# Two bottleneck blocks in one kernel: Winograd streams that build each unit when it is due, and two more idle matmuls around each Gram stage

## The chip, the cores and the metric

The kernel runs on one core of one Trainium2 chip. The metric is the device time of one execution, in microseconds. It was taken from three runs before the change. One further execution was recorded by the hardware profiler, and all durations below come from that one unless a sentence says otherwise.

## The reference, cut to what matters

Two residual blocks follow each other. Each has three convolutions with batch normalisation over the whole batch of 64 images of 14 x 14 pixels; everything is float32.

```python
def block(x, w1, b1, g1, be1, w2, b2, g2, be2, w3, b3, g3, be3, residual_scale):
    out = relu(bn(conv(x,   w1, b1, pad=0), g1, be1))    # 1x1, 1024 -> 256 channels
    out = relu(bn(conv(out, w2, b2, pad=1), g2, be2))    # 3x3,  256 -> 256
    out =      bn(conv(out, w3, b3, pad=0), g3, be3)     # 1x1,  256 -> 1024
    return relu(x + softplus(residual_scale) * out)
x = block(x, *layer0); x = block(x, *layer1)             # x: (64, 1024, 14, 14)
```

## The kernel before, in words

Images are taken two at a time; such a pair is a tile `t`, 0 to 31, with 392 pixels per channel. The 256-channel activations stay in SBUF (`y_all`). The 1024-channel input of a block is streamed in tiles `x` (128 partitions x 8 x 392 values, 1568 KB each): from the kernel's input in block 0, from a DRAM copy `mid` in block 1.

The span has these stages, in order:

1. The first 1x1 convolution of block 0 (`first`, 0 to about 300 us). Beside it, VectorE and ScalarE transform the 3x3 filters of both blocks (`filters`), whose raw weights come by DMA (L194).
2. The 3x3 convolution of block 0 (`conv2`, about 300 to 590 us). It ends with `busy(psum, "m", 6)` on L968: six matmuls of the identity with 448 columns, whose result nobody reads. They occupy TensorE while the other engines finish the batch statistics.
3. The Gram stage of block 0 (`gram`, `conv3_stats`, about 590 to 690 us). The statistics of the third convolution come from the 256 x 256 Gram matrix of the activations, so the convolution needs no pass of its own for them. The activations are normalised in pieces by ScalarE (L546) and shifted by VectorE (L994). The first seven chunks of 256 pixels are transposed by TensorE (`by_tensor`, L1024) and copied to SBUF by VectorE (L1030); the others by DMA and VectorE.
4. The third convolution of block 0 fused with the first of block 1 (`fused`, about 690 to 1270 us).
5. The 3x3 convolution of block 1, ended by the same six idle matmuls (about 1270 to 1560 us), and its Gram stage (about 1560 to 1650 us).
6. The last third convolution with the residual sum and the stores (`final`, about 1650 us to the end).

The 1x1 convolutions use a scheme of seven block products instead of eight (class `Seven`, one object a *unit*). `p1` to `p7` are the products on TensorE. They go into PSUM banks `y`, `x`, `p` with a prefix `a` or `c` for the first or third convolution, so `cp` is the bank `p` of a third convolution. `after1` to `after7` are what VectorE, ScalarE and GpSimd do with a bank after its product. One bank `p` is used twice by one unit: `p5` starts it, `after5` adds it to the tile (L466), `p3` accumulates further into it, `after3` adds it again (L466).

`stream` (L300) interleaves the units. In the steady state TensorE does `p1` of a unit, `p3` and `p4` of the unit before, then `p6`, `p2`, `p5`, `p7` of this unit. `stream` holds one unit ahead: at the head of its loop it asks the generator for the `following` unit before the current one is done (L306), and so knows which one is the last.

The generators do work when they are asked for a unit:

- In `final` (L1141), one pair of tiles `t, t+1` has four units (q = 0 to 3). Before q = 0 the generator makes the four operand sums `ct0` to `ct3` on VectorE (`column_sums`, L423): L430, L431, L432, L433. After a unit was taken it calls `go_out` of an older one. That is a relu on VectorE (L522) and two stores of 392 KB on SyncE's queue (L525), one from each of the two tiles. After q = 1 it loads the next tiles `x` (L1159), up to tile `t + 4`. Five `x` buffers exist, so a load waits until all four stores of the tile that held the buffer have landed.
- `fused` (L1167) runs two streams in lock step, `first_convs` and `last_convs`; the latter makes the sums and loads one tile per four units.
- The first stage (L1345) loads two tiles per unit.

The order of work is partly fixed. Every matmul, the relus of `go_out` and some others are held in program order on their engine (`tc.keep_in_program_order`). Everything else, among it the additions of L466, the sums `ct` and all DMA issues, is placed by the framework's scheduler, which takes the position in the program as priority. Each engine and each DMA issuing queue then works through its list in order.

Of the kernel before, what the change touches and what calls it, by code (L numbers as in the profile page):

```python
# [45 lines left out]
CS = C // P  # L46
MS = M // P
G = 2
T = N // G
# [38 lines left out]
def bottlenecks(ctx: ExitStack, tc: tile.TileContext, x, w1s, w2s, w3s, pars, out):  # L88
# [208 lines left out]
            yield from self.p3()  # L297
            yield from self.p4()

    def stream(items, beside=lambda: None):  # L300


        before, items = None, iter(items)
        now = next(items)
        while now is not None:
            following = next(items, None)  # L306
            yield from now.p1()
            if before is not None:
                beside()
                yield from before.last()  # L310
                beside()
            else:
                yield from now.p2()
            yield from now.p6()
            if before is not None:
                before.end()
                if following is not None:
                    beside()
                    yield from now.p2()
            beside()  # L320
            yield from now.p5()
            beside()
            yield from now.p7()
            beside()
            if following is None:
                yield from now.p2()
            before, now = now, following
        yield from before.last()
        before.end()

# [225 lines left out]
    def conv2(psum, pool, b, par, aff, affine_of, stats):  # L556

        order = (1, 2), (3, 4), (NF - 1, 0)
        pairs = [(g, p) for g in range(NG) for p in order]
# [392 lines left out]
        for k in range(NG * NF):  # L952
# [12 lines left out]
            item.columns(*qs)  # L965
            finished.send(item)
            queue = queue[1:] + list(itertools.islice(made, 1))
        busy(psum, "m", 6)  # L968

    def conv3(psum, t, o, w3, tag=None):  # L970
        ps = psum.tile(tag=tag)
# [6 lines left out]
    def gram(psum, pool, homes, aff, minus_c, beside):  # L978

        g0, g1 = psum.tile(M + 1, "cp"), psum.tile(P + 1, "ap")
        zts = [pool.tile([P, CH, M + 1], FP, tag=f"zt{i}", name=f"zt{i}") for i in range(NZT)]
        for zt in zts:
            nc.gpsimd.memset(zt[:, :, M:], 1.0)
        zts = itertools.cycle(zts)

        head = 3 * CH * P
        start = FIRST * CH * P
        bounds = [0, CH * P, head, head + STEP, *range(2 * GPX, NPX + 1, GPX)]  # L990
        pieces = list(zip(bounds, bounds[1:]))

        def less(s, y):
            tc.keep_in_program_order(nc.vector.tensor_scalar(y, y, minus_c[:, s : s + 1], None, ALU.add))  # L994

        def norm_to(end):

            while pieces and pieces[0][0] < end:
                a, e = pieces.pop(0)
                for s in reversed(range(MS)):  # L1000
                    y = y_all[:, s, a:e]
                    if a == 0 and s == 1:
                        norm_vector(s, y, aff, minus_c[:, s : s + 1])
                    else:
                        norm(s, y, aff)
                        less(s, y)

        def spread(k):

            first = start + k * STEP if k else head  # L1010
            norm_to(first + STEP)
            x = homes[k % 2][:, : MS * STEP].rearrange("p (s j f) -> p s j f", s=MS, j=4)
            for i, j in itertools.product(range(4), range(4)):
                queue = nc.gpsimd if 4 * i + j in (1, 3, 6, 8, 10, 13, 15) else nc.sync
                a = first + i * RUN
                queue.dma_start(out=x[32 * i : 32 * i + 32, :, j], in_=y_all[32 * j : 32 * j + 32, :, a : a + RUN])
            return x.rearrange("p s j f -> p (s j) f")

        def by_tensor(a):
            tp = psum.tile(CH * M)  # L1020
            for c in range(CH):
                for s in range(MS):
                    tc.keep_in_program_order(
                        nc.tensor.transpose(  # L1024
                            tp[:, (c * MS + s) * P : (c * MS + s + 1) * P],
                            y_all[:, s, a + c * P : a + (c + 1) * P], ident,
                        )
                    )
            zt = next(zts)
            tc.keep_in_program_order(nc.vector.tensor_copy(zt[:, :, :M], tp.rearrange("p (c m) -> p c m", c=CH)))  # L1030
            return zt

        def by_vector(x, i):
            zt = next(zts)
            tc.keep_in_program_order(
                nc.vector.transpose(
                    zt[:, :, :M].rearrange("p b (n c) -> p b n c", c=32),
                    x[:, :, i * CH * 32 : (i + 1) * CH * 32].rearrange("p n (b r) -> p b n r", r=32),
                )
            )  # L1040
            return zt

        def pairs():

            norm_to(head)
            then = {
                1: lambda: ready.append(spread(0)),
                2: partial(norm_to, 2 * GPX),
                4: partial(norm_to, 3 * GPX),
                5: lambda: ready.append(spread(1)),  # L1050
            }
            for i in range(FIRST):
                a = i * CH * P
                yield by_tensor(a if a < head else a + STEP)
                if i in then:
                    then[i]()
            for k in range(STEPS):
                x = ready.pop(0)
                for i in range(RUN // (CH * 32)):
                    yield by_vector(x, i)  # L1060
                if k + 2 < STEPS:
                    ready.append(spread(k + 2))
            norm_to(NPX)
            for i in range(LAST):
                yield by_tensor(NPX - (LAST - i) * CH * P)

        ready = []
        total = NPX // (CH * P)
        before = None
        for k, zt in enumerate(itertools.chain(pairs(), (None,))):  # L1070
            if before is not None:
                for c in range(CH):
                    first, last = k == 1 and c == 0, k == total and c == CH - 1
                    matmul(g0, before[:, c, 0:P], before[:, c, :], start=first, stop=last)
                    matmul(g1, before[:, c, P:M], before[:, c, P:], start=first, stop=last)
            before = zt
            if k in beside:
                beside[k]()
        return g0, g1
# [61 lines left out]
    def final(psum, pool, xpool, xs, a, w3, aff):  # L1141


        units = []

        def pairs():
            for t in range(1, T - 1, 2):
                ys = [[two(t + i, s) for i in range(2)] for s in range(MS)]
                sums = column_sums(pool, ys, PX)
                for q in range(CS // 2):  # L1150
                    units.append(Conv3Pair(psum, pool, xs[t : t + 2], q, PX, ys, sums, w3, aff, out[t : t + 2]))
                    yield units[-1]

                    while len(units) > 2:
                        units.pop(0).go_out()
                    if q == 1:

                        for i in range(len(xs), min(t + 5, T)):
                            xs.append(load_x(xpool, 1, i))  # L1159

        for _ in stream(pairs()):
            pass
        for unit in units:
            unit.go_out()
        residual(psum, xs[T - 1], 1, T - 1, a, aff)

    def fused(psum, pool, xpool, xs, w1, w3, aff, par, stats, one_done):  # L1167

        def last_convs():
            for t in range(1, T):
                if t + 1 < T:
                    xs.append(load_x(xpool, 0, t + 1))
                ys = [[two(t, s)[:, i * H // 2 : (i + 1) * H // 2] for i in range(2)] for s in range(MS)]
                n = PX // 2
                sums = column_sums(pool, ys, n)
                for q in range(CS // 2):
                    yield Conv3(psum, pool, xs[t], q, n, ys, sums, w3, aff, mids[t] if q == CS // 2 - 1 else None)

        def first_convs():
            for t in range(T):
                yield Conv1(psum, pool, xs[t : t + 1], (t,), w1, par, stats, one_done)

        a, c = stream(first_convs()), stream(last_convs())
        for i in range(LAG):
            next(c)
        while True:
            more = next(a, "end"), next(c, "end")
            if more == ("end", "end"):  # L1190
                break
# [122 lines left out]
    with tc.tile_pool(name="first", bufs=1) as one, tc.tile_pool(  # L1314
        name="first_x", bufs=4
    ) as xpool, ExitStack() as scope:
        psum = Psum(scope, ["ps"], ps=4, ay=2)
# [29 lines left out]
                xs = [load_x(xpool, 0, t + i) for i in range(2)]  # L1347
                yield Conv1(psum, one, xs, (t, t + 1), w1, par[0], stats1, one_done)

        for _ in stream(items(), beside):  # L1350
            pass

    for b in range(2):
# [95 lines left out]
```

## Time and profile before

| | |
|---|---|
| median of 3 runs | 1959.65 us (1957.53 to 1960.48) |
| profiled execution, its own time | 1959.24 us |
| its span, first to last instruction | 1957.5 us |
| TensorE clock granted over the span | 0.998 |
| busy: PE, weight load, DVE, ACT, POOL | 98%, 82%, 79%, 53%, 27% |
| PE idle: 0 to 300, 300 to 590, 590 to 700 us | 1.6, 6.6, 5.2 us |
| PE idle: 700 to 1260 us | 0.0 us |
| PE idle: 1260 to 1560, 1560 to 1670, 1670 to 1957.5 us | 8.8, 4.8, 10.6 us |

PE is TensorE's matmul, DVE is VectorE, ACT is ScalarE, POOL is GpSimd, SP is SyncE, which here only issues DMAs. Idle PE is the length of the stretch less the busy time in it. A float32 matmul appears as one or more PE records, and a line of the timeline merges equal ones that follow each other: "x2" is two records. Duration and distance are two things: a matmul of 128x392 is busy for 0.49 us, but the next one starts 0.33 us after it, because they overlap.

### The profile page before, as it was taken

What the parts mean: (1) busy time and instruction counts of PE and PEld (TensorE: products, weight loads), DVE (VectorE), ACT (ScalarE), POOL (GpSimd) and SP (SyncE); (2) the same over time, 40 slices, a digit from 0 to 9 for tenths busy, and PEclk for the clock granted to TensorE, in tenths of its full rate; (3) what the DMA queues carried; (4) which work ended last, traced back from release to release, by engine and by line L of the source; (5) the groups of instructions that cost most, each with busy time, mean ns of one, the idle gap of its engine ahead of it and who ended that gap; (6) DMA issues with size and microseconds to landing.
All of it is one profiled execution on the core that took longest, in us unless ns stands there. A gap on an engine that the chain in (4) does not pass through costs nothing.

```text
span 1957.5 us, 26989 instructions
## 1 busy us (share of the span) xinstructions
PE 1919.9 (98%) x9430; PEld 1614.4 (82%) x9430; DVE 1552.4 (79%) x2491; ACT 1041.5 (53%) x2082; POOL 532.0 (27%) x638
## 2 busy tenths in 40 slices
PE   9999999999999999999999999989999999999998
PEld 5555558999997799999999999989999887555554
DVE  5778768999998667676776776699999976888786
ACT  2222214677775055555555555457777641666665
POOL 0111100000105133433433333301010051666664
PEclk9999999999999999999999999999999999999999
DMA  7766635576747634444444444257667386899997
GB/s 289 278 248 254 249 112 165 178 208 191 207 142 203 198 135 187 173 165 177 182 169 165 179 184 166 99 183 204 203 192 207 124 199 232 298 322 339 336 341 264
DMA packets 188983, 408.39 MB, mean 209 GB/s; under 512 B 24944, under 2 KB 165136, under 8 KB 172336
## 3 DMA queue, kind: packets, MB, share of 16 engines
q1 hardware_dynamic: 161728, 324.66, 48.5%
q0 software_dynamic: 21504, 30.94, 6.9%
q10 hardware_dynamic: 5616, 51.06, 6.3%
q8 instruction: 75, 1.23, 0.3%
q14 instruction: 60, 0.49, 0.1%
HBM read 263.75 MB, written 115.34 MB: 194 GB/s over the span
## 4 chain that ended last, share of the span: by engine, by line
PE 90%; DVE 7%; issue 1%; ACT 1%; DMA 1%; SPq 0%; POOL 0%; DVEq 0%
PE ay L168 17%; PE cy L168 16%; PE columns L168 13%; PE cp L168 12%; PE ap L168 10%; PE m L168 6%; PE l L168 6%; PE ax L168 4%; PE cx L168 4%; PE ps L168 1%; DVE x L466 1%; DVE ct L431 1%; DVE f L801 0%; DMA home<-y 0%; DVE ct L433 0%
## 5 line engine op out<-in xcount | busy, mean ns | idle before, releaser
L333 ACT ACTIVATE cu<-cy,scale 128x196 f32<-128x196 f32 (+1 forms) x552 | 257.7, 473 | 286.7 <-PE cy L168 279.6
L168 PE MATMUL columns<-v,ub 128*128 128x224 f32 (+1 forms) x1536 | 301.1, 337 | 0.7 <-ACT columns L760 0.7
L168 PEld LDWEIGHTS columns<-v,ub 128*128 128x128 f32 x1536 | 269.4, 188 | 4.1 <-ACT columns L760 1.2
L333 ACT ACTIVATE x<-x,shift 128x392 f32<-128x392 f32 x428 | 239.7, 613 | 55.1 <-POOL x L492 53.2
L466 DVE SCALAR_TENSOR_TENSOR x<-cp,scale,x 128x196 f32<-128x196 f32 (+1 forms) x368 | 178.1, 484 | 98.0 <-PE cp L168 96.4
L168 PE MATMUL cy<-ct,ws 128*128 128x196 f32 (+1 forms) x736 | 222.0, 383 | 1.1 <-ACT cu L333 1.1
L168 PE MATMUL ay<-at,ws 128*128 128x196 f32 (+1 forms) x752 | 209.2, 381 | 0.0
L487 POOL TENSOR_TENSOR x<-x,cu 128x196 f32<-128x196 f32 (+1 forms) x184 | 159.2, 865 | 174.1 <-ACT cu L333 162.5
L492 POOL TENSOR_TENSOR x<-x,cu 128x392 f32<-128x392 f32 x124 | 125.9, 1015 | 192.8 <-DVE x L466 188.1
L168 PEld LDWEIGHTS ay<-at,ws 128*128 128x128 f32 x752 | 136.4, 190 | 33.6 <-ACT au L333 0.5
L168 PEld LDWEIGHTS cy<-ct,ws 128*128 128x128 f32 x736 | 133.4, 190 | 36.4 <-ACT cu L333 3.8
L168 PE MATMUL m<-sums,ua 128*128 128x224 f32 (+1 forms) x752 | 147.6, 340 | 6.2 <-DVE sums L624 6.2
L168 PE MATMUL l<-diffs,ub 128*128 128x224 f32 (+1 forms) x768 | 149.7, 338 | 3.0 <-PE columns L168 2.9
L513 POOL TENSOR_TENSOR x<-x,cu 128x392 f32<-128x392 f32 x120 | 124.5, 1038 | 86.1 <-DVE x L466 79.2
L871 POOL DMA_DIRECT2D y<-f x24 | 31.1, 1532 | 412.8 <-DVE f L801 320.8
L168 PEld LDWEIGHTS l<-diffs,ub 128*128 128x128 f32 x768 | 133.6, 189 | 7.0 <-PE columns L168 5.9
L168 PEld LDWEIGHTS m<-sums,ua 128*128 128x128 f32 x752 | 132.2, 191 | 8.7 <-DVE sums L624 7.9
L466 DVE SCALAR_TENSOR_TENSOR x<-cx,scale,x 128x196 f32<-128x196 f32 (+1 forms) x184 | 89.3, 485 | 59.1 <-PE cx L168 58.2
L333 ACT ACTIVATE au<-ay 128x196 f32<-128x196 f32 (+1 forms) x141 | 53.6, 380 | 152.0 <-PE ay L168 149.3
L168 PE MATMUL cx<-y,w 128*128 128x196 f32 (+1 forms) x404 | 124.1, 392 | 0.4 <-DVE x L1130 0.4
L168 PE MATMUL cy<-y,w 128*128 128x196 f32 (+1 forms) x404 | 123.8, 392 | 0.0
L168 PE MATMUL cp<-zt 128*128 128x257 f32 x392 | 118.8, 385 | 1.8 <-DVE zt L1030 1.7
(211 smaller groups left out, 3950.1 us busy)
## 6 DMA issues: line engine op xcount, KB each, us to landing
x<-in_x SPq DMA_DIRECT2D x62, 1568.0 KB, 6.8
ub<-u SPq DMA_DIRECT2D x94, 768.0 KB, 5.0
x<-mid SPq DMA_DIRECT2D x32, 1568.0 KB, 8.6
mid<-x ACTq DMA_DIRECT2D x31, 1568.0 KB, 5.1
out<-x SPq DMA_DIRECT2D x123, 392.0 KB, 6.5
ua<-u SPq DMA_DIRECT2D x94, 256.0 KB, 3.0
u<-y POOLq DMA_DIRECT2D x48, 256.0 KB, 5.9
home<-y SPq DMA_DIRECT2D x90, 96.0 KB, 4.2
```

The source lines that it names most:

```text
L168: tc.keep_in_program_order(nc.tensor.matmul(*args, **kw))
L333: tc.keep_in_program_order(nc.scalar.activation(*args, **kw))
L431: nc.vector.tensor_add(t2, t3, ys[0][0])
L466: nc.vector.scalar_tensor_tensor(v, bank, self.scale[:, o : o + 1], v, ALU.mult, ALU.add)
L487: nc.gpsimd.tensor_add(self.part(1, 1), self.part(1, 1), u3)
L492: nc.gpsimd.tensor_add(v, v, self.u12)
L513: nc.gpsimd.tensor_add(v, v, self.u12[:, i * self.n : (i + 1) * self.n])
L871: nc.gpsimd.dma_start(out=out_rows[0][:, o], in_=f[:, o], accum_op=ALU.add)
```

## The change

`stream` no longer holds a unit ahead. It gets the number of units as an argument and counts, so it still knows the last one; a unit, and all that its generator does before it, is made when the one before is finished. The order of the products on TensorE in a stream stays the same. Apart from that, `conv2` ends with seven idle matmuls instead of six, and the Gram stage has one idle matmul after its first chunk of transposes, into the otherwise unused bank `ax`. Both are in each of the two blocks: four idle matmuls more in all.

```diff
-    def stream(items, beside=lambda: None):
-        before, items = None, iter(items)
-        now = next(items)
-        while now is not None:
-            following = next(items, None)
+    def stream(items, total, beside=lambda: None):
+        before = None
+        for k, now in enumerate(items, 1):
             yield from now.p1()
             if before is not None:
                 beside()
...
             yield from now.p6()
             if before is not None:
                 before.end()
-                if following is not None:
+                if k < total:
                     beside()
                     yield from now.p2()
             beside()
...
             beside()
-            if following is None:
+            if k == total:
                 yield from now.p2()
-            before, now = now, following
+            before = now
         yield from before.last()
         before.end()
...
-        busy(psum, "m", 6)
+        busy(psum, "m", 7)
...
                 yield by_tensor(a if a < head else a + STEP)
+                if i == 0:
+                    busy(psum, "ax", 1)
                 if i in then:
...
-        for _ in stream(pairs()):
+        for _ in stream(pairs(), (T // 2 - 1) * CS // 2):
...
-        a, c = stream(first_convs()), stream(last_convs())
+        a, c = stream(first_convs(), T), stream(last_convs(), (T - 1) * CS // 2)
...
-        for _ in stream(items(), beside):
+        for _ in stream(items(), T // 2 - 1, beside):
```

## The prediction

> **What bounds the kernel now.** I read the busy table first, then the stretches by stage, then the waits of TensorE (PE) in the stage where it has any, and last the chain of waits and the timelines around one such wait. PE is the bound at 98%, so only its idle time can be won.
>
> ```profile
> PE 1919.9 (98%) x9430; PEld 1614.4 (82%) x9430; DVE 1552.4 (79%) x2491; ACT 1041.5 (53%) x2082; POOL 532.0 (27%) x638
> core 0: us, PE busy (x) PEld busy (x) DVE busy (x) ACT busy (x) POOL busy (x), PEclk, DMA share, GB/s
> 700.00:1260.00 560.00, 560.00 (x3379) 560.00 (x3378) 393.71 (x873) 307.32 (x723) 216.22 (x242) 1.00 0.43 167
> 1700.00:1920.00 220.00, 215.24 (x647) 121.64 (x646) 177.57 (x276) 146.57 (x277) 143.30 (x139) 1.00 0.95 334
> 594.70:598.20 3.50, 3.43 (x13) 2.96 (x14) 3.08 (x5) 3.50 (x4) 0.00 (x0) 0.55 0.62 231
> ```
>
> In the fused stage PE is never idle, so nothing is to be won there. In the final stage it is idle for 4.8 of 220 us, beside DMA engines at 0.95. The last row is the begin of the first Gram stage, where the granted clock was 0.55. From 1670 us on, the waits of PE have a single line:
>
> ```profile
> PE cp L168 <- DVE x L466: 6.1, 14, 0.4
> ```
>
> Fourteen waits of 0.43 us, one for each change from a pair of tiles to the next. The chain of waits shows one of them, and VectorE's timeline what follows:
>
> ```profile
> 1746.84 0.67 PE cy L168 x2
> 1747.52 0.02 issue
> 1747.54 0.84 DVE ct L431
> 1748.38 0.02 issue
> 1748.40 0.57 DVE ct L433
> 1748.97 0.54 DVE x L466
> 1749.50 0.47 DVE ct L432
> 1749.98 0.55 DVE x L466
> 1750.52 0.04 issue
> 1750.57 0.93 PE cp L168 x2
> ```
>
> ```profile
> 1750.43 0.64 DVE L522 TENSOR_SCALAR x<-x,shift 128x392 f32<-128x392 f32 x1
> 1750.99 1.37 DVE L430 TENSOR_TENSOR ct<-y 128x392 f32<-128x392 f32 x1
> 1752.29 0.61 DVE L466 SCALAR_TENSOR_TENSOR x<-cp,scale,x 128x392 f32<-128x392 f32 x1
> ```
>
> `p3` of the old pair's last unit (1750.57) waits for `after5`, the L466 that reads the same bank `cp`. This stands on VectorE behind three sums for the new pair (L431, L433, L432) and another L466. Without the wait `p3` would start at 1749.31 (the `p1` before it) + 2 x 0.33 = 1749.97. It loses 0.60, and its first matmul, after the pause, 0.10 more (0.43 instead of 0.33 to the second). So one boundary costs 0.70 and the fourteen 9.8 us; this is the most that the final stage can give.
>
> [...]L430 took 1.37 us beside GpSimd's L487 (1750.81 to 1751.94), the equally large L433 0.57 us with GpSimd idle. [...]stores issued behind two loads land about 1.1 us apart after them. [...]Here it was 0.55 after pauses of only 1.19 and 0.67 us[...]. At the second Gram stage, with the same pauses, the clock stayed at 1.00, so this is not certain in each execution.
>
> **The change, part by part.** The base is the profiled execution, 1959.24 us (span 1957.5, 1.7 around it); the median of the runs is 0.4 above it.
>
> *The sums in `final`.* The built order of VectorE after the change is, at each boundary: L431, L433, L466, **L466 of `after5`**, L522, **L432**, L430, L466. Before it was L431, L433, L466, **L432**, L466 of `after5`, L522, L430, L466. Only L432 moves, by two places. It held its queue for 0.47 us (1749.50 to 1749.98 in the chain). So `after5` and with it `p3` come 0.47 earlier: 1750.10 instead of 1750.57, with 0.13 of wait left plus the 0.10. Gain 14 x 0.47 = 6.6 us. L432 is a new wait for `p5` of the new unit: it ends at about 1751.1, `p5` starts at 1753.30 - 0.47 = 1752.83, so 1.7 to spare. Behind L430 the sum on VectorE is the same, and the L466 of `after3` stays at 1752.29 while PE is 0.47 ahead. Next in line is the following unit's `after5` (1754.16 before). The L466s from 1752.29 on can follow each other at 0.53 us: 1752.29, 1752.82, 1753.35, 1753.88; the last lets `p3` go 0.68 later (as 1749.89 to 1750.57), at 1754.56, and PE wants it at 1755.28 - 0.47 = 1754.81. There is 0.25 to spare, so this holds, but barely.
>
> *The relus, stores and loads in `final`.* `go_out` moves from the begin of unit k+2 to the begin of unit k+3, one unit or 4.61 us later (`p1` to `p1`, 1759.23 to 1763.84), with everything behind it on SyncE: two stores per unit and, per pair, two loads. What may suffer is the arrival of the tile first needed in the next pair. Before: loads issued at 1760.93 and 1761.51, landing 6.7 and 11.3 us later; the first is read by the `after5` of the next pair at 1773.30, so it has 5.7 to spare. A shift by a whole unit leaves 5.7 - 4.61 - 0.47 = 0.6. In the built order the store just ahead of the loads is now one that needs no L522, so SyncE gets to the load at once and it waits for the old tile's last store only. That is issued 0.97 after `p1` of the third unit and lands 3.1 later (as the store at 1760.22): 1763.3. The load lands at 1763.3 + 6.7 = 1770.0, or with two stores still ahead of it on the rings 1771. Spare: 1.8 us or more. Load on the rings per pair: two loads 4.4 + 4.9 and eight stores of 1.1 make 18.1 us; a period of 19.13 becomes 18.66, so there is room for it, at a share of 0.97. Cost taken: 0. Bounds: below nothing there is no gain, as no PE wait on a load exists; above, see the rivals.
>
> *The end.* One more relu (0.6) and two stores fall among the last units. From 1935 us on no loads run and stores land 3 us after issue; the last store belongs to the tile 31 and follows PE. Cost 0, at most 0.6.
>
> *`fused` and the first stage.* In `fused` L432 (0.36 us) moves from 811.69 to about 812.4 in the tile that I looked at, its reader `p5` starts at 815.80, and PE has no wait. In the first stage two filter loads go ahead of one tile load on SyncE. They are 590 KB each, 1.4 us on the rings, and the tile has over 5 us to spare. Both 0.
>
> *Idle matmuls.* Here is the first Gram stage:
>
> ```profile
> 587.60 4.69 PE L168 MATMUL m<-ident 128*128 128x448 f32 x12
> 593.48 0.63 PE L1024 MATMUL cy<-ident,y 128*128 128x128 f32 x4 [1.19 <-issue]
> 594.77 0.92 PE L1024 MATMUL ay<-ident,y 128*128 128x128 f32 x4 [0.67 <-DVE y L994]
> 595.49 1.12 PE L168 MATMUL cp<-zt 128*128 128x257 f32 x2
> 598.71 0.60 PE L168 MATMUL cp<-zt 128*128 128x257 f32 x2
> ```
>
> Six idle matmuls take 4.69, one 0.78 us. The seventh ends at 593.07, under the pause to 593.48: free. The one in `ax` starts at 594.1 and ends at 594.9, 0.1 past 594.77: 0 to 0.1, and the later waits for L994 (0.70, in the second stage 1.42) take that up. What they may bring: the four products from 595.49 to 598.12 took 2.63 us, where equal ones at full clock took about 1.3. Of that 1.3 only 0.54 can reach the next wait, since VectorE's copy of the next chunk (598.91) could not start before its L994 ends (598.37). Range 0 to 0.54, taken 0.3 for the first stage and 0 for the second.
>
> Sum: 6.6 + 0.3 = 6.9 us. 1959.24 - 6.9 = 1952.3; against the median **1952.7 us**.
>
> **Rivals.** 0.2% of the time, 3.9 us, is about what a measurement of this kernel can tell from no change.
>
> *A, the wait goes (0.64):* 1952.7, with 1949 if the whole 0.70 goes and 1955.5 if half of 0.47 does.
>
> *B, VectorE and GpSimd collide (0.18):* L432 now stands directly before L430, and GpSimd runs two additions there (L513 1749.65, L487 1750.81). If both sums take 1.37 instead of one, everything behind comes 0.8 later: `after5` of the next unit at 1754.68, `p3` at 1755.36 against 1754.81 wanted. That stall of 0.55 eats the gain: 1959, between 1956 and 1960. For it speaks the 1.37; against it that GpSimd's two additions have the time for only one such block.
>
> *C, nothing moves (0.08):* another wait, such as ScalarE's copy before `p6` (0.47 to spare before), takes the place at once: 1959.5.
>
> *D, the tiles come late (0.10), slower:* the loads land behind their reader. Each us of lateness stops `p3` at every boundary. The gain is gone at 0.47 us late; at 1.0 late the time is 1959.2 - 6.6 + 14 x 1.0 = 1967. That needs a first load issued after about 1767, or stores that land 3 us later than now. For it speaks the DMA share of 0.95; against it the sum of 18.1 in 18.66.
>
> **How the numbers follow.** A and a small part of B are faster by over 0.2%: 0.68. The rest of B, C and the edge of A are within: 0.21. D and its neighbours: 0.11. The range of 8 in 10 goes from 1950.0 (nearly all waits gone and the clock too) to 1958.5 (most of B in it), and leaves out D.
>
> **What would show it.** Right: the waits of `cp` for L466 after 1670 us fall from 6.1 to about 2 us (14 x 0.13), `p1` to `p1` over a pair from 19.13 to 18.66, the chain of waits has no L432, and the clock in the first Gram stage stays near 1.00. B would show as L432 and L430 both above 1 us; D as waits of L466 for a load from `mid`. I am wrong in the main step if the final stage is not at least 4 us shorter.

## The result, and the profile after

The median after the change is 1953.35 us (1952.55 to 1956.07), against 1959.42 (1957.53 to 1960.48) for the kernel before beside it, ten runs each. The ratio is 0.9973, 95% interval 0.9964 to 0.9983: 5.3 us faster, between 3.3 and 7.1. The prediction was 1952.7. The profiled execution of after took 1952.55 us with a span of 1950.8, so 6.7 less than the profiled execution of before. The table says where these 6.7 lie; each landmark is the start of a TensorE (PE) instruction in the two traces. The first stretch begins with the first of them, at 1.06 us, and the last ends with the span.

| stretch, up to | before, us | after, us | difference | predicted |
|---|---|---|---|---|
| first stage, to the first product of `conv2` | 303.94 | 303.48 | -0.46 | 0 |
| `conv2`, block 0, to its last product | 282.40 | 281.16 | -1.24 | 0 |
| Gram stage, block 0, to the last `cp<-zt` | 77.82 | 77.35 | -0.47 | -0.3 |
| `fused`, to the first product of `conv2` | 610.44 | 610.45 | 0 | 0 |
| `conv2`, block 1 | 281.73 | 281.81 | +0.08 | 0 |
| Gram stage, block 1 | 77.48 | 77.59 | +0.11 | 0 |
| `final`, to the last product in `cp` | 306.38 | 301.65 | **-4.73** | -6.6 |
| the last tile | 16.21 | 16.21 | 0 | 0 |

First the busy table and the stretches of after (columns as before the change: length, busy time of the engines, granted clock, DMA share, GB/s).

```profile
PE 1921.3 (98%) x9438; PEld 1611.9 (83%) x9438; DVE 1556.5 (80%) x2491; ACT 1041.8 (53%) x2082; POOL 529.7 (27%) x638
1700.00:1920.00 220.00, 220.00 (x657) 122.01 (x656) 184.66 (x282) 148.56 (x282) 143.18 (x141) 1.00 0.95 336
593.00:596.50 3.50, 3.50 (x23) 3.03 (x23) 3.09 (x5) 3.50 (x3) 0.00 (x0) 1.00 0.63 225
```

PE is now never idle by this view in 220 us of `final`, where it lacked 4.8. The list of waits of PE has no line left after 1670 us (before: 6.1 us in 14 waits). Yet `final` is only 4.73 shorter, not 9.8. The chain of waits at a boundary between two pairs shows where the rest is (start, length up to the next piece, what):

```profile
1745.54 1.32 PE cy L168 x4
1746.86 0.88 PE cp L168 x2
...
1750.37 1.31 PE cy L168 x4
1751.69 0.81 PE cp L168 x2
```

Two matmuls in a row without a pause take 0.66 in this list. The `p3` of the old pair takes 0.88, and the `p3` of the next unit, 4.8 us later, 0.81. Neither pause is long enough to be listed as a wait, and L432 (now L430) is gone from the chain. So each boundary still loses 0.22 at the first place and **0.15 at a second one that was not there before**. Before, it lost 0.70 at one place. That is 0.33 net per boundary; the second stall stands behind 13 of the 14 boundaries, so 14 x 0.48 less 13 x 0.15 makes 4.8. From pair to pair PE's period went from 19.13 to 18.80 us.

VectorE's timeline of after at this boundary, and GpSimd's beside it, tell what the second place waits for:

```profile
1746.14 0.62 DVE L464 SCALAR_TENSOR_TENSOR x<-cp,scale,x 128x392 f32<-128x392 f32 x1
1746.67 0.93 DVE L520 TENSOR_SCALAR x<-x,shift 128x392 f32<-128x392 f32 x1
1747.53 1.37 DVE L430 TENSOR_TENSOR ct<-y 128x392 f32<-128x392 f32 x1
1748.82 0.56 DVE L428 TENSOR_TENSOR ct<-y 128x392 f32<-128x392 f32 x1
1749.30 0.62 DVE L464 SCALAR_TENSOR_TENSOR x<-cp,scale,x 128x392 f32<-128x392 f32 x1
1749.84 0.61 DVE L464 SCALAR_TENSOR_TENSOR x<-cy,scale,x 128x392 f32<-128x392 f32 x1
1750.37 0.61 DVE L464 SCALAR_TENSOR_TENSOR x<-cx,scale,x 128x392 f32<-128x392 f32 x1
1750.90 0.61 DVE L464 SCALAR_TENSOR_TENSOR x<-cp,scale,x 128x392 f32<-128x392 f32 x1
```

```profile
1746.37 1.02 POOL L511 TENSOR_TENSOR x<-x,cu 128x392 f32<-128x392 f32 x1 [1.71 <-DVE x L464]
1747.34 1.14 POOL L485 TENSOR_TENSOR x<-x,cu 128x392 f32<-128x392 f32 x1
```

The order is the predicted one: `after5` (1746.14), the relu L520, `t1` (L430), `t3` (L428). Four L464 follow without a gap, and the last of them, the next unit's `after5`, ends at 1751.51. Its `p3` should start at 1751.53 (0.66 after the `p1` at 1750.87) and starts at 1751.57. The blocks behind `after5` are not those of before: L520 takes 0.93 here instead of 0.64. The 1.37 has moved from `t3` to `t1`, and `t3` has the 0.56 that `t1` had.

### The profile page after: what moved, and what is told of

Its sections match the earlier page's. It is cut to its first block, busy times and chain, and to the rows that moved or that the text cites. A ratio compares the mean times of both kernels' runs of the same rounds, so it can differ in the third digit from the quotient of the medians.

```text
span 1950.8 us, 26996 instructions
## 1 busy us (share of the span) xinstructions
PE 1921.3 (98%) x9438; PEld 1611.9 (83%) x9438; DVE 1556.5 (80%) x2491; ACT 1041.8 (53%) x2082; POOL 529.7 (27%) x638
## 4 chain that ended last, share of the span: by engine, by line
PE 90%; DVE 6%; issue 1%; ACT 1%; DMA 1%; SPq 0%; POOL 0%; DVEq 0%; ACTq 0%
PE cy L168 17%; PE ay L168 17%; PE cp L168 12%; PE columns L168 12%; PE ap L168 10%; PE m L168 6%; PE l L168 6%; PE cx L168 5%; PE ax L168 4%; PE ps L168 1%; DVE f L799 1%; ACT y L544 1%; DVE steps L697 0%; DMA home<-y 0%; DVE v L628 0%
## 5 line engine op out<-in xcount | busy, mean ns | idle before, releaser
L464 DVE SCALAR_TENSOR_TENSOR x<-cp,scale,x 128x196 f32<-128x196 f32 (+1 forms) x368 | 178.2, 484 | 97.0 <-PE cp L168 95.9
L464 DVE SCALAR_TENSOR_TENSOR x<-cx,scale,x 128x196 f32<-128x196 f32 (+1 forms) x184 | 89.2, 485 | 57.4 <-PE cx L168 57.4
```

What stands on the lines that cost most here:

```text
L464: nc.vector.scalar_tensor_tensor(v, bank, self.scale[:, o : o + 1], v, ALU.mult, ALU.add)
```

## Experiments

Line numbers of kernels with the change are two lower (L466 is L464, L432 is L430, L522 is L520). "Final" is the length of the stretch `final` in the table above, read from each kernel's profiled execution.

| kernel | median, us | ratio to before, 95% interval | final, us |
|---|---|---|---|
| sums_only | 1953.6 | 0.9973 (0.9963 to 0.9984) | 301.67 |
| relus_only | 1958.61 | 0.9999 (0.9991 to 1.0007) | 306.41 |
| idle_only | 1958.8 | 0.9998 (0.9990 to 1.0006) | 306.44 |
| final_only | 1955.08 | 0.9980 (0.9973 to 0.9988) | 302.30 |
| first_only | 1959.72 | 1.0001 (0.9993 to 1.0009) | 306.40 |
| relu_scalar | 1954.58 | 0.9974 (0.9964 to 0.9984) | 301.98 |
| third_later | 1952.44 | 0.9965 (0.9952 to 0.9979) | 299.73 |
| spread | 1949.72 | 0.9952 (0.9940 to 0.9965) | 297.81 |
| spread_cover | 1948.61 | 0.9944 (0.9932 to 0.9957) | 297.14 |
| spread_early | 1947.68 | 0.9942 (0.9929 to 0.9954) | 296.58 |

The kernel before had a median of 1958.57 beside the first four kernels, 1959.48 beside first_only, relu_scalar, spread and spread_cover, and 1959.1 beside the other two.

### Which part carries the gain

**sums_only** is after, with the relus, stores and loads put back by one unit.

```diff
-                    while len(units) > 2:
+                    while len(units) > 1:
                         units.pop(0).go_out()
-                    if q == 1:
+                    if q == 0:
```

> The kernel after with the relus, stores and loads of the final stage put back one unit (issued as early as in the kernel before); the sums of a new pair stay late. The built order of VectorE, PE, ScalarE and GpSimd is that of the kernel after, only SyncE differs. Theory (the gain comes from L430, the third sum, leaving the queue ahead of the product's addition of after5): the same time as after, 1953 to 1954 us, 5 to 6 below before, with a boundary wait of PE of about 0.12 and a second small stall of about 0.15 in the next unit. Rival 1 (the gain comes from stores and loads shifting in time): 1958 to 1960, as before. Rival 2 (VectorE's relu L520 grew from 0.64 to 0.93 us because the DMA traffic around it shifted): L520 falls back to 0.64 behind the boundary, the second stall goes, 1951 to 1952.

**relus_only** is after, with the sums made one unit ahead again.

```diff
...
+            coming = sums_of(1)
             for t in range(1, T - 1, 2):
-                sums = column_sums(pool, ys, PX)
+                ys, sums = coming
                 for q in range(CS // 2):
+                    if q == CS // 2 - 1 and t + 2 < T - 1:
+                        coming = sums_of(t + 2)
```

> The kernel after with the sums of a new pair created one unit ahead again, so that L430 stands ahead of after5 on VectorE as in the kernel before; the relus, stores and loads stay one unit late. Theory: the wait of 0.43 at each of 14 boundaries is back and with it 4.7 us: about 1958, no more than 1 or 1.5 us below before (what the idle matmuls and the first stages give). Rival 1 (stores and loads give the gain): 1953 to 1954.

These two split the change in `final` in two, and the answer has no overlap. With the late sums alone the whole gain is there (301.67 us, 0.9973). With the late relus, stores and loads alone there is none (306.41 us, 0.9999), and the old wait is back to the digit:

```profile
PE cp L168 <- DVE x L464: 6.1, 14, 0.4
```

So the gain of `final` comes from the one sum that leaves the queue ahead of `after5`. Rival 2 of sums_only falls too: the second stall stays when the stores and loads go back.

**final_only** is before, with the late stream in `final` alone; **first_only** is its complement, with the late stream in the first stage and `fused`. **idle_only** is before with the two idle matmuls per block. The edit of first_only is against after and takes the idle matmuls out as well; `stream_late` and `stream_ahead` are copies of the new and the old `stream`.

```diff
 # final_only
-        for _ in stream(pairs()):
+        for _ in stream_late(pairs(), (T // 2 - 1) * CS // 2):
 # first_only
-        for _ in stream(pairs(), (T // 2 - 1) * CS // 2):
+        for _ in stream_ahead(pairs()):
 # idle_only
-        busy(psum, "m", 6)
+        busy(psum, "m", 7)
...
+                if i == 0:
+                    busy(psum, "ax", 1)
```

> The kernel before with the late stream in the final stage alone; fused and first stage keep the unit ahead, and no idle matmul is added. Theory (the final stage carries 4.7 of the gain, the idle matmuls up to 0.5, fused and first stage nothing): 1954.2 to 1955. Rival (the first stage's or fused's order gives part, 0.5 to 1.7 us by the landmarks of the two traces): 1955 to 1956.5.

> The kernel before with the new stream in the first stage and in the fused stage alone; the final stage keeps the unit ahead, no idle matmul added. Theory (nothing in fused or first stage; the 1.1 us that conv2 of the first block was shorter in after is a clock that happened to fall in before): as before within 1 us, each stage up to the final one with the same length as before but for the clock; the fall at 345 us may come or not. Rival (the new order of the first stage is what keeps the clock up at 345 us, as it did in three of three executions): no fall at 345 us, 1.1 us below before, 1957.5.

> The kernel before with only the two more idle matmuls per block. Theory: the granted clock in the first Gram stage no longer falls to 0.55, and the stage from the last product of conv2 to the last product of the Gram stage is 0.3 to 0.5 us shorter in an execution where the clock had fallen, 0.0 to 0.1 longer where it had not: 1959 us, within 1 us of before. Rival (the idle matmuls keep the clock up beyond the Gram stage and give a large part of the 5 us): 1955 to 1957.

final_only keeps 4.08 us of the 4.73 in `final` and lies at 0.9980. The 0.65 that it lacks stand at two boundaries, where PE stops for 0.44 (before 1867.56) and 0.30 us (before 1905.42) in the second stall instead of 0.04. At the first of them `after5` had waited for a tile:

```profile
DVE x L466 <- DMA x<-mid: 0.3, 1, 0.3
```

What held the second is not shown. first_only is the kernel before in time (1.0001), and its `fused` takes 610.45 us as in all the others. So those two stages give nothing, as predicted. For the times of idle_only the edit is too small; its effect is read from the stage below.

### The clock: a part with a cause and a part by chance

The Gram stage of block 0 in after, TensorE's timeline:

```profile
585.90 5.45 PE L168 MATMUL m<-ident 128*128 128x448 f32 x14
591.79 0.63 PE L1022 MATMUL cy<-ident,y 128*128 128x128 f32 x4 [0.44 <-PE m L168]
592.25 0.92 PE L168 MATMUL ax<-ident 128*128 128x448 f32 x2
598.46 0.66 PE L1022 MATMUL cy<-ident,y 128*128 128x128 f32 x4 [1.43 <-DVE y L992]
```

The pauses of 1.19 and 0.67 us are now one of 0.44 (the seventh idle matmul fills most of the first, `ax` the second), and the stretch behind them runs at 1.00 instead of 0.55. The wait for L992 behind it grew from 0.70 to 1.43: most of what the products gain is lost there again, as the prediction had it. All three profiled executions without the idle matmuls (before, final_only, first_only) show the clock down here, and none of the nine with them. The stage took 77.96 us on average in the three (77.82, 77.93, 78.12) and 77.52 in the nine (77.26 to 77.80). So where the clock would have fallen, the idle matmuls are worth 0.44 us, on predicted bounds of 0 to 0.54. In block 1 the same pauses stand in the three, the clock fell in none of them, and the stage took 77.57 us on average in the three and 77.55 in the nine: nothing gained.

`conv2` of block 0 is another matter. There PE pauses for about 2.61 us at about 343 us, waiting for VectorE's L624, in all kernels but spread_cover and spread_early, and behind that pause the clock is halved in some executions (0.50 from 346 to 348 us in idle_only and third_later, 1.00 in after).

It fell in five profiled executions (before, idle_only, final_only, first_only, third_later) and not in five others (after, sums_only, relus_only, relu_scalar, spread). After four kernels the new stream of the first stage looked like its cause, since it fell in none that had it; first_only and third_later have the new stream and show the fall. So the 1.24 us that after is shorter here belongs to the execution, not to the change.

The traces show how the pause lay beside the changes of the clock. In before the granted clock rises to 1.00 at 4.51 us and is 0.50 from 345.84, 595.02 and 1956.93 us, which is 100, 173 and 572 times 3.413 later; in after, from 5.85 to its one fall at 1951.45, behind the last matmul, it is 570 times. The first two falls of before last 3.41 us each. So I counted the idle PE in windows of 3.41 us laid from the rise, which comes at another place in each of the two. Here are two windows of third_later, parted at its fall, then two of after:

```profile
342.19:345.60 3.41, 1.20 (x7) 0.83 (x5) 3.41 (x8) 1.43 (x4) 0.00 (x0) 1.00 0.61 224
345.60:349.01 3.41, 3.01 (x8) 2.76 (x9) 3.41 (x5) 0.00 (x0) 0.00 (x0) 0.50 0.00 0
340.35:343.77 3.42, 2.51 (x14) 2.13 (x12) 3.42 (x8) 1.43 (x4) 0.00 (x0) 1.00 0.74 248
343.77:347.18 3.41, 1.70 (x9) 1.71 (x10) 3.41 (x6) 0.29 (x1) 0.00 (x0) 1.00 0.03 12
```

In third_later 2.21 us of the pause lie in one window, and the clock is 0.50 in the next. In before it is 2.52 (342.43 to 345.84), with 0.50 in the next as well. In after the end of a window cuts the pause into 0.91 and 1.71, and the clock stays at 1.00. In the first Gram stage the two short pauses of before lie in one window (591.60 to 595.02) and make 1.86 together, with the fall behind it; in block 1 the end of a window cuts the second of them, no window of before has more than 1.49 there, and the clock stays at 1.00. Up to the last matmul no other window of before has more than 1.64 us of idle PE and none of after more than 1.71, and no fall follows any of these. All this is read from the traces afterwards; no run moved the pauses against the clock, so it is not shown that this decides.

spread_cover (below) fills this pause with three idle matmuls:

```diff
+            if k == NF - 1:
+                busy(psum, "m", 3)
             for v in more:
                 v.start()
```

> The kernel spread with three more idle matmuls (0.78 us each, 2.3 together) in the pause of 2.6 us that TensorE has in conv2 before the first product of the second group (345 us and 1315 us). Theory (whether the clock halves after a pause of this length is chance: it fell at 345 us in three profiled executions and not in three others, and cost 1.1 us where it fell): no execution with the fall, median 0 to 1 us below spread and fewer runs with a mean clock below 1.000. Rival (the idle matmuls hold up the product behind them): 0.2 to 0.5 us per block slower than spread.

`conv2` took 281.06 us there and 281.08 in spread_early, as in the executions without a fall, and the product behind is not held up. Fewer runs with a mean clock below 1.000 were expected, and that came: none of five in spread_cover, all five in spread. But the profiled execution of spread, without a fall before its end, is among the 0.999, so this figure says little. The gain in the median, 1.1 us, is about what two medians of five runs each can differ by. The fall came in neither of the two profiled executions with this pause filled; it is absent from five of ten without that.

### What is left at a boundary

**third_later** is after with one VectorE instruction moved: `t3` of the coming pair is made in the last unit of the pair before.

```diff
...
+            coming = third(1)
             for t in range(1, T - 1, 2):
-                sums = column_sums(pool, ys, PX)
+                ys, t3 = coming
                 for q in range(CS // 2):
+                    if q == 3 and t + 2 < T - 1:
+                        coming = third(t + 2)
```

> The kernel after with one sum moved: the t3 of a coming pair (0.56 us, L428 in after) is made in the last unit of the pair before, behind that unit's L520, and no longer behind t1 at the boundary. Nothing else differs on any engine. Theory (behind the boundary VectorE's queue is 0.29 longer than my sum had it, because L520 grew from 0.64 to 0.93 beside GpSimd; that leaves the next after5 some 0.05 late, which with a first matmul of 0.43 after the pause costs 0.15): the second stall goes, the stage to the last cp is about 14 x 0.15 = 2.1 shorter than after (301.65), 299.5, and the time 1951 to 1952; the boundary's own 0.12 + 0.10 stays or shrinks. Rival (the second stall is not VectorE's queue): 301.6 and 1953 to 1954. Rival 2 (t3 grows to 1.37 in its new place beside GpSimd and makes the boundary's after5 late instead): boundary stall 0.4 or more, 302 to 306.

`final` took 299.73 us, 1.92 less than after (expected 2.1); the median, 1952.44, lies just above the 1951 to 1952 expected. The L464 of `after3` now starts 2.78 us after the `p1` of the boundary (1750.05 - 1747.27) instead of 3.26, and there is no second stall in any pair; the first stays, with 0.12 + 0.10. VectorE's timeline:

```profile
1747.90 0.93 DVE L520 TENSOR_SCALAR x<-x,shift 128x392 f32<-128x392 f32 x1
1748.75 1.38 DVE L1161 TENSOR_TENSOR ct<-y 128x392 f32<-128x392 f32 x1
1750.05 0.61 DVE L464 SCALAR_TENSOR_TENSOR x<-cp,scale,x 128x392 f32<-128x392 f32 x1
```

L520 and `t1` are as long as in after; only `t3` no longer stands behind them (in after 0.48 of the queue). So it is the length of VectorE's queue that made the second stall, and it was too long by less than this.

**relu_scalar** takes L520 off VectorE and gives it to ScalarE.

```diff
-            tc.keep_in_program_order(nc.vector.tensor_scalar(v, v, self.shift[:, o : o + 1], 0.0, ALU.add, ALU.max))
+            act(v, v, AF.Relu, bias=self.shift[:, o : o + 1])
```

> The kernel after with the relu L520 of go_out on ScalarE instead of VectorE. Theory (at a boundary VectorE's queue is too long by a fraction of a us: L520 0.93 beside t1 1.37, so the next unit's after5 is late and PE stops a second time for about 0.15): with 0.6 to 0.9 us taken off that queue the second stall goes, 14 x 0.15 = 2.1 us less than after: about 1951. The boundary wait of 0.12 + 0.10 at p3 itself stays, since L520 stands behind that after5. Rival 1 (the second stall comes from the bank or from TensorE itself, not from VectorE's queue): 1953 to 1954, the second stall of 0.15 still there. Rival 2 (ScalarE's copies ahead of p6 come late instead, they had 0.47 to spare before): PE waits for ScalarE in each unit, slower than after, 1956 or more.

It missed on the time: `final` took 301.98, 0.33 more than after, and the median is 1954.58. The second stall at `p3` is gone at all boundaries but one, as the theory says, but a stall of the same size stands behind it, at `p6` of the same unit, for a copy of ScalarE that now has the relu ahead of it. ScalarE's and TensorE's timelines:

```profile
1752.09 0.61 ACT L331 ACTIVATE x<-x,shift 128x392 f32<-128x392 f32 x1
1752.60 0.57 ACT L331 ACTIVATE cu<-cy,scale 128x392 f32<-128x392 f32 x1
1753.22 0.93 PE L168 MATMUL cy<-ct,ws 128*128 128x392 f32 x2
```

`p6` is due at 1753.15 (1752.49 + 0.66) and starts at 1753.22, behind the copy that ends at 1753.17; with the slow first matmul that is 0.17 again, at 12 boundaries. At the thirteenth `p3` is late after all (1902.55), behind an `after5` that starts 0.18 us after its tile has landed. Rival 2, ScalarE late in its turn, holds at the boundaries, not in each unit. And the queue of VectorE lost the 0.93 of L520 but became only 0.27 shorter: the L464 of `after3` starts 2.99 after the `p1` of the boundary (1749.34 - 1746.35) instead of 3.26. Both sums behind `after5` now ran long, 1.13 and 1.38.

**spread** takes the heap apart. The four sums have two buffers each and are made one per unit.

```diff
...
+                    v = pool.tile([P, PX], FP, tag=f"ct{i}", name=f"ct{i}", bufs=2)
...
                 for q in range(CS // 2):
+                    if q == 1 and t + 2 < T - 1:
+                        steps = sums_of(t + 2)
+                        coming = next(steps)
+                    for ins in itertools.islice(steps, 1):
+                        tc.keep_in_program_order(ins)
```

> The kernel after with the four sums of a pair in two buffers each and made one per unit during the pair before, behind that unit's L520; only VectorE's order differs. Theory (all that is left at a boundary, 0.22 at p3 and 0.15 in the next unit, is VectorE's sums in a heap): both stalls go, 14 x 0.37 = 5.2 us less than after, 1948 to 1949, period of a pair 18.43. Rival 1 (a sum of 1.37 beside GpSimd in each unit makes after5 late four times a pair instead of once): PE waits of 0.1 to 0.3 in most units, 56 x 0.1 = 5.6 to nothing gained or slower, 1953 to 1959. Rival 2 (the transfers, with a DMA share of 0.91, become the bound at the shorter period): waits of L464 for loads, gain below 3 us.

Both stalls went at all but three boundaries; `final` took 297.81 us, 3.84 less than after instead of 5.2, and the median, 1949.72, lies above the 1948 to 1949 expected. VectorE now waits for loads seven times; this list had no such wait in after, and one of 0.3 us in final_only and of 0.7 in relu_scalar:

```profile
DVE x L464 <- DMA x<-mid: 4.7, 7, 1.0
```

So rival 2 holds in kind, though the gain is above its 3 us.

**spread_early** is spread_cover with relus, stores and loads put back by a unit, the edit of sums_only.

> The kernel spread_cover with the relus, stores and loads of the final stage put back one unit, as early as in the kernel before. In spread and spread_cover VectorE's L464 waited 4.0 to 4.7 us in all for loads (x<-mid), and in after not at all. Theory (these waits come from loads issued one unit late now that the period is short, and they lie within the slack of after5 but for one or two): the waits for loads go, the stage to the last cp falls from 297.14 to 296.6 or 296.9, the time 1948 to 1948.6. Rival (the DMA engines are full at a share of 0.95, the place of issue does not matter): waits for loads remain, 297.1 and the same time.

The waits for loads are gone, and with them the last stalls: `final` 296.58 us, 9.80 below before, which is the 14 x 0.70 that the prediction gave as the most this stage can yield. The rival of spread_early falls: with the same stores and loads issued earlier, the stretch below carried a share of 0.98 without a wait of VectorE or PE for them.

```profile
1700.00:1920.00 220.00, 220.00 (x670) 127.00 (x669) 176.16 (x286) 151.57 (x287) 159.91 (x144) 1.00 0.98 349
```

At 1947.68 us it is the fastest version here, 0.9942 (0.9929 to 0.9954) of before, though this interval does not tell it from spread_cover's 0.9944.

## Why the prediction was right, and where its sum was off

*The main step.* `p3` of the old pair was released 0.48 earlier against its own `p1` (0.70 lost before, 0.22 after; predicted 0.47, with "0.13 of wait left plus the 0.10"). relus_only and sums_only show that the one sum is its cause. The text said that less than 4 us in `final` would prove it wrong; it was 4.73.

*The term that was mis-sized: "0.25 to spare, so this holds, but barely".* It did not hold. The sum behind it kept `after3` at 2.98 us after the `p1` of the boundary (1752.29 - 1749.31); it came at 3.26 (1749.30 - 1746.04). The 0.28 is L520's growth from 0.64 to 0.93. The prediction had moved L522 ahead with `after5`, with its old length. But GpSimd's addition beside it hardly moved: it starts 0.34 after `p1` before and 0.33 after. Before, L522 began 0.78 us into it and ended 0.22 behind its end (1751.07 and 1750.85). Now it begins 0.30 into it and ends 0.21 behind its end (1747.60 and 1747.39). The relu of the next unit, 1.21 us long, ends 0.22 behind another (1752.64 and 1752.42), and the usual one of 0.81 in spread 0.23 behind (1746.14 and 1745.91). All 57 relus of after from 1665 to 1930 us, and all 55 of before, end 0.21 to 0.23 us after the GpSimd addition that was running when they began, whenever that was. Why they do is not shown.

The end of the long sum behind the relu goes the same way: it comes 0.42 after GpSimd's next addition, in before (L430, 1752.36 and 1751.94) as in after (1748.90 and 1748.48). So the prediction's step "Behind L430 the sum on VectorE is the same" fails, because the ends in this part of the queue went with GpSimd's and were no sum of fixed lengths. The instructions that ran under GpSimd gained little from an earlier start, and what stood behind them added its whole length. To take `t3` away from behind them gave its 0.48 (third_later); to take away the relu, one of them, gave only 0.27 of its 0.93 (relu_scalar).

*What a miss costs.* The next `after5` was late by some 0.04 us only. PE paid 0.15, since the first matmul after a pause took 0.43 to the second instead of 0.33, behind the 0.04 here as behind the 0.60 of before. I had counted these 0.10 at the old wait, and not as the price of a new one. 6.6 less 13 x 0.15 is 4.65, against 4.73 measured.

*Rival B* had the right engines and the wrong victim. `t1` and `t3` did not both take 1.37 in after; one such block passed from `t3` to `t1`. The argument that GpSimd's two additions have the time for only one such block does not hold, though: in relu_scalar the sums took 1.13 and 1.38. In after the first addition caught the relu instead, the third instruction there, and I had not asked what becomes of it. Its result, a stall at the next `p3`, came at 0.15 instead of 0.55.

*Rival D, tiles too late.* In after the first load of a pair lands at 1767.17 and its first reader follows at 1769.70 (1750.90 + 18.80), 2.5 to spare; the prediction had 1.8 or more. That is this pair only: from 1826 us on it is between 0.4 (landed 1863.33, read 1863.73) and 1.2, so the sum was too generous. Lateness did not occur in the profiled execution of after. It did once in final_only, which has the same `final` (0.3 us), and at the shorter period of spread the same order made VectorE wait 4.7 us for loads.

*The first stage, `fused` and the end* cost nothing, as said; that the first stage was 0.46 shorter is within the 303.39 to 304.41 that twelve profiled executions show, those with the old stream among both the short and the long ones.

*Gram stages.* 0.44 where the clock would have fallen and nothing in block 1, against 0.3 and 0: right in kind, a little more than taken. That it fell in all three executions without the idle matmuls in block 0, and in none in block 1, was measured; in before the pauses made 1.86 us in one window in block 0 and at most 1.49 in block 1.

*Sum.* 4.73 + 0.44 = 5.2 us is what the profiles put down to the change, the 0.44 only in an execution where the clock would have fallen; the ratio gives 5.3. The prediction's 6.9 against the profiled execution, 6.7 in the two profiles, agrees by luck: 1.9 too much in `final` was made up by a clock that fell in `conv2` in one of the two executions and by the first stage's own variation.

## What to carry to other kernels

Where the trace shows instructions of one engine ending at a fixed distance behind those of another (here 0.21 to 0.23 and 0.42 to 0.43 us behind a GpSimd addition), and an instruction moves ahead of them, they need not come earlier by as much: work out beside which instruction of the other engine each of them then runs, and take its end from that one's end. A slack that comes out within 0.3 us, after several durations from one execution, is no slack; price the miss at its fixed cost, here 0.10 for the restart of TensorE plus the lateness. And where a few instructions are heaped at one place because of single buffers, spreading them with a second buffer gave a shorter `final` (296.58 to 297.81 us) than the orders of the heap that were tried (299.73 to 302.30).

## What the runs showed of the hardware

- In before the granted clock was 0.50 for 3.41 us from 345.84 and from 595.02 us, behind 3.41 us with 2.52 and 1.86 us of idle PE. In after it stayed at 1.00 up to the last matmul, with at most 1.71 us of idle PE in a window of that length. A pause of 2.61 us was followed by a fall in five executions of ten; `conv2` took 282.40 us with the fall in before and 281.16 without it in after. With three idle matmuls in the pause the clock fell in neither of two executions.
- The restart of TensorE cost 0.10 us after a pause of 0.04 (after) as after one of 0.60 (before): the first 128x392 matmul took 0.43 to the next one instead of 0.33.
- A relu of 128x392 on VectorE took 0.64 to 1.21 us in before and after, and ended 0.21 to 0.23 us after the GpSimd addition that ran when it began, in 112 of 112 cases. A sum of two inputs that began with GpSimd idle took 0.55 to 0.57 us there, and one that began under a GpSimd addition ended 0.42 or 0.43 after that one's end, in 56 of 56 cases.
